# A graph layer on one core: order of the first loads, place of the weight transforms, one load and one sum on other engines

## The chip, the core and the metric

The kernel runs on one core of a Trainium2 chip. A core has TensorE (PE, with weight loads shown apart as PEld), VectorE (DVE), ScalarE (ACT), GpSimd (POOL) and SyncE (SP), all running their own instruction streams in order and waiting for each other by semaphores. DMA transfers are issued from SP, ACT and POOL. The metric is the device time of one execution in microseconds (us), as the median of several runs; lower is better.

## The reference, cut to what is computed

```
h = relu(layernorm(x))                        # x: 32 x 512 x 256 float32, adj: 32 x 512 x 512
hc = relu(bn(conv1d(h, conv1_w, width 1)))    # over channels
x_conv = relu(bn(conv1d(hc, conv2_w, width 17)) + h)
s = h @ w_se.T + b_se                         # 3 numbers per node
A = exp(-|s_n - s_m|^2) * adj
x_nmp = A @ relu(h @ w_msg.T + b_msg)
gi = [x_conv, x_nmp] @ w_ih.T + b_ih          # 3*256 outputs: r, z, n
gh = h @ w_hh.T + b_hh
r, z = sigmoid(gi_r + gh_r), sigmoid(gi_z + gh_z)
out = x + (1 - z) * tanh(gi_n + r * gh_n) + z * h
```

## The kernel before, in words

The 32 batches are worked in two groups of 16 (`GB`). Each group has a first part and a nodes part, and after both groups the gates follow for 16 pairs of batches.

**First part** (`first_part`). For each batch: load x; row statistics on VectorE (`statistics`, L375 to L380) and a power on GpSimd (L381); `normalise` (L394, on VectorE in group 0 and mostly in group 1); `transpose_h`, eight transposes on TensorE (phT, L402) and relu out of PSUM (L406), with a store to DRAM (hd, L407); `conv1` (pc, L422) with the batch norm's shift added on VectorE (L425) and a relu on ScalarE (L426); and `windows_to_freq` (px, L437), which takes the batch before into the frequency domain, because the 17 wide convolution is done by Fourier transforms over windows of 64 tokens. In program order a batch b does the statistics of b + 2, the transposes of b + 1, xn of b + 2, conv1 of b and px of b - 1.

In group 0 the weights of that convolution are transformed as well, in 32 steps of `weights_to_freq`. A step is four matmuls (pw, L346) of 17 x 80 weights and 512 columns, one on each group of 32 rows of the array, whose four PSUM banks are copied to tiles wst by ScalarE (L356) and VectorE (L354). After every second step four stores (wd, L360) go out on SP. Four steps share a tile w2p of taps, of which there are two buffers, filled by `load_taps` (L333, L334), from GpSimd's queue after the first. Which steps a batch does, and where, `between` says: it hands out a list for each of three places, before `normalise`, behind `conv1` and behind px. In the kernel before, a batch from 2 on has one step at the first place and one at the second; batch 6 has a third one behind px; batch 0 has two behind its conv1, and batch 1 one.

`between` also issues one entry of the list `load_weights` per batch, from batch 1 on: the back matrix of the inverse transform (L296), the message weights and biases, the vectors (`load_vectors`, L236, and `vectors`, L242 to L254 on GpSimd) and a scaling on GpSimd (L293).

All PSUM tiles come from one ring of eight banks (`bank`), in program order: a new tile waits until the tile eight places before has been read.

The order of each engine is the program's own (`manual_schedule`). Each DMA transfer from SP and ACT takes the next of eight semaphores in turn, and its issue waits until the transfer that had the semaphore before has landed. In the kernel before, x_0 comes in four transfers, two on SP and two on ACT, after vec on ACT; then on SP four of w1 (L199), x_1 (L203), five of the taps; and on ACT taps and fwd (L1267, L1268).

**Group 1's first part** has no weight transforms. Instead it finishes four frequency units of group 0 (the list `left`, at five places called `fill`), and combines the gate weights (`combine_weights`, shown at L1236): a list of steps, one per batch from batch 17 on, each with sums on GpSimd and copies on ScalarE. The first step only loads w_hhT (four transfers on SP, L199); the second, at the next batch, reads it.

**Nodes part** (`nodes`): messages (pm, L537), the affinity matrix and its product with the messages (pn, L641 and L624), and the products in the frequency domain (py, L486).

**Gates.** Before the first pair, sums of blocks of the operands are made on GpSimd in the order `FIRST_ORDER` (`block_sum`, L782 and L784): those of part hn, then `inverse(0)`, which brings the convolution back (pc, L844) and leaves cp, and then those of part c, the first of which is t4, a difference of rows of cp into tnc. The product (pg, L879) `t4_1` is the fourth of the first pair and reads it.

The places that the change touches most are these:

```python
load_weights = [
    partial(nc.sync.dma_start, back, nc.inline_tensor(back_np, name="dft_back").ap()),
    partial(load_rows, wmsg[:, :, :D], w_msgT, nc.sync),
    ...
n = (3, 0, *(3 if b == 6 else 2 for b in range(2, GB)))[b]
mine = [[steps.pop(0)] for _ in range(n)]
if b % 2 == 0 and b // 2 + 1 < QI // PI:
    mine[b > 0].insert(0, partial(load_taps, gen, b // 2 + 1))
return (mine[0] + mine[1], mine[2:]) if b == 0 else mine
```

Of the kernel before, what the change touches and what calls it, by code (L numbers as in the profile page):

```python
# [15 lines left out]
P = 128  # L16
# [134 lines left out]
def gnn_layer(  # L151
# [15 lines left out]
    nc = tc.nc  # L167
# [5 lines left out]
    NC = N // P  # L173
    G = 3 * D
    W = N // V
    GB = P // W
# [113 lines left out]
    def scale_embedding():  # L290
# [2 lines left out]
            nc.gpsimd.tensor_scalar(t, t, float(np.sqrt(2.0)), None, op0=ALU.mult)  # L293

    load_weights = [
        partial(nc.sync.dma_start, back, nc.inline_tensor(back_np, name="dft_back").ap()),  # L296
        partial(load_rows, wmsg[:, :, :D], w_msgT, nc.sync),
        partial(load_rows, wmsg[:, :, D:], w_seT, nc.sync),
        partial(nc.sync.dma_start, bmsg[:, :D], b_msg.to_broadcast([P, D])),
# [1 line left out]
        load_vectors,  # L301
        vectors,
        scale_embedding,
    ]


# [370 lines left out]
    def combine_weights():  # L677

        steps, loads, begins = [], [], []
        for k, src in enumerate((w_hhT, w_ihT[D:], w_ihT[:D])):  # L680
# [1 line left out]
                       for n, m in ((4, G // 2), (9, P), (len(PRODUCTS) + 2, P)))  # L682
            rows = w.rearrange("p (c h) m -> p c (h m)", c=DC)
            load = (partial(nc.sync.dma_start, rows, src.rearrange("(c p) m -> p c m", p=P)) if k == 1 else
                    partial(load_rows, rows, src, nc.sync))
            steps.append([])

            a11, a21, a12, a22 = (
# [76 lines left out]
    def block_sum(p, name, part):  # L765
        if name in BLOCK_SUMS:
            x, op, y = BLOCK_SUMS[name]
            dst, x, y = (operand(p, v, part) for v in (name, x, y))
            op = ALU.add if op == "+" else ALU.subtract
        else:  # L770
            rows = list(PAIR_SUMS)

            def whole(v):
                if isinstance(v, int):
                    return CP[p][:, v] if part == "c" else HN[p][:, :, v]
                return TNC[0][:, rows.index(v)] if part == "c" else TN[0][:, rows.index(v)]

            (x, y), op = PAIR_SUMS[name], ALU.subtract
            dst, x, y = whole(name), whole(x), whole(y)
            if part == "hn":  # L780
                for k in range(2):
                    nc.gpsimd.tensor_tensor(dst[:, k], x[:, k], y[:, k], op=op)  # L782
                return
        nc.gpsimd.tensor_tensor(dst, x, y, op=op)  # L784

    def sums_ahead(p, part):
        for name in SUMS_AHEAD:
# [464 lines left out]
    with tc.tile_pool(name="freq", bufs=1) as fpool:  # L1252
# [3 lines left out]
        with phase("first", "gen"):  # L1256
            gen = pools["gen"]
            per = N // D
            steps = [partial(weights_to_freq, gen, pc, i) for pc in range(QI // PI) for i in range(0, PI, per)]

            X[0] = pools["first"].tile([P, NC, D], FP, tag="x", name="x_0", bufs=3)
            for c in range(NC):
                (nc.sync if c % 2 == 0 else nc.scalar).dma_start(X[0][:, c, :], x[0, c * P : (c + 1) * P, :])
            load_w1()
            load_x(1)
            load_taps(gen, 0, nc.sync)
            nc.scalar.dma_start(taps, nc.inline_tensor(taps_np, name="dft_taps").ap())  # L1267
            nc.scalar.dma_start(fwd, nc.inline_tensor(fwd_np, name="dft_fwd").ap())  # L1268

            def between(b):  # L1270
                if 1 <= b <= len(load_weights):
                    load_weights[b - 1]()

                n = (3, 0, *(3 if b == 6 else 2 for b in range(2, GB)))[b]
                mine = [[steps.pop(0)] for _ in range(n)]
                if b % 2 == 0 and b // 2 + 1 < QI // PI:
                    mine[b > 0].insert(0, partial(load_taps, gen, b // 2 + 1))
                return (mine[0] + mine[1], mine[2:]) if b == 0 else mine

            with tc.manual_schedule():  # L1280
                xf = first_part(0, freq_tile, between)
# [109 lines left out]
        with phase("pw", "ahead"):  # L1391
            with phase("seven", "nodes"):
                with tc.manual_schedule():
                    nodes(0, xf, range(UNITS - LEFT), GB, range(UNITS - LEFT, UNITS - LEFT + 2))
            with phase("first", "sums"):
                combine = combine_weights()

                def between(b):

                    if b == GB - 3:  # L1400
                        for u in range(3):
                            load_unit(1, u)
                    two = [partial(sum_unit, pools["pw"], 1, b - GB + 3)] if b - GB + 3 >= REAL else []
                    return combine[b - 1] if 0 < b <= len(combine) else [], two


                pw, (u0, u1, u2, u3) = pools["pw"], range(UNITS - LEFT, UNITS)
                left = [[partial(load_unit, 0, u2, pools["sums"]), partial(prepare, pw, 0, u1, xf)],
                        [partial(product, pw, 0, u0, xf), partial(prepare, pw, 0, u2, xf)],
                        [partial(product, pw, 0, u1, xf), partial(load_unit, 0, u3)],  # L1410
                        [partial(prepare, pw, 0, u3, xf), partial(product, pw, 0, u2, xf)],
                        [partial(product, pw, 0, u3, xf)]]
                prepare(pw, 0, u0, xf)
                with tc.manual_schedule():
                    xf = first_part(1, freq_tile, between, left)
            with phase("seven", "nodes"):
                with tc.manual_schedule():
                    nodes(1, xf, range(UNITS), GB - 3)
# [92 lines left out]
```

## Time and profile before

| | before |
|---|---|
| median of 3 runs (range), us | 1768.27 (1766.25 to 1769.55) |
| profiled execution: time, us | 1769.15 |
| its span, first to last instruction, us | 1767.4 |
| mean granted clock of TensorE | 0.996 |
| TensorE busy, us (share) | 1752.5 (99%) |
| VectorE, ScalarE, GpSimd busy, us | 1338.3, 674.4, 1110.6 |
| first part of group 0, until the last px ends, us | 161 |
| first part of group 1, from its first transposes to the last px, us | 436 to 552 |
| first gate product, us | 844 |

The profile is of one execution. A line of the timeline gives the start and the length of a run of like instructions in us, the engine (SPq, ACTq and POOLq issue DMAs), the line of the kernel, the operation, what it writes and reads, how many, and in brackets how long the engine had been idle and what ended that. TensorE's matmuls overlap, so the start of one run of matmuls to the start of the next is the better measure of what it costs than the length shown.

### The profile page before, as it was taken

What the parts mean: (1) busy time and instruction counts of PE and PEld (TensorE: products, weight loads), DVE (VectorE), ACT (ScalarE), POOL (GpSimd) and SP (SyncE); (2) the same over time, 40 slices, a digit from 0 to 9 for tenths busy, and PEclk for the clock granted to TensorE, in tenths of its full rate; (3) what the DMA queues carried; (4) which work ended last, traced back from release to release, by engine and by line L of the source; (5) the groups of instructions that cost most, each with busy time, mean ns of one, the idle gap of its engine ahead of it and who ended that gap; (6) DMA issues with size and microseconds to landing.
All of it is one profiled execution on the core that took longest, in us unless ns stands there. A gap on an engine that the chain in (4) does not pass through costs nothing.

```text
span 1767.4 us, 24501 instructions
## 1 busy us (share of the span) xinstructions
PE 1752.5 (99%) x8046; PEld 1355.0 (77%) x8046; DVE 1338.3 (76%) x2617; ACT 674.4 (38%) x1543; POOL 1110.6 (63%) x1086
## 2 busy tenths in 40 slices
PE   9999999999999999999999999999999999999998
PEld 6777888888898888886877787778777787778754
DVE  7885888877896778876487778777877688777867
ACT  4556545543446445444322232323223232323221
POOL 3341786888554788777867556755766566755551
PEclk9999999999999999999999999999999999999999
DMA  8998988995778988888523553345423552345333
GB/s 230 317 299 230 259 216 236 232 240 175 257 267 213 260 229 238 227 239 275 177 67 64 120 126 95 75 81 125 117 66 69 126 126 72 68 111 125 102 60 71
DMA packets 311314, 295.16 MB, mean 167 GB/s; under 512 B 146940, under 2 KB 240668, under 8 KB 310804
## 3 DMA queue, kind: packets, MB, share of 16 engines
q1 hardware_dynamic: 301012, 265.77, 56.9%
q0 software_dynamic: 6736, 25.86, 4.6%
q10 hardware_dynamic: 3440, 1.97, 0.4%
q8 instruction: 64, 1.05, 0.2%
q14 instruction: 62, 0.51, 0.1%
HBM read 194.39 MB, written 99.16 MB: 166 GB/s over the span
## 4 chain that ended last, share of the span: by engine, by line
PE 94%; DMA 2%; DVE 1%; POOL 1%; SPq 1%; ACT 0%; issue 0%; ACTq 0%; POOLq 0%; DVEq 0%
PE pg L879 28%; PE pn L896 16%; PE py L486 12%; PE pn L641 10%; PE pm L537 6%; PE pc L422 5%; PE pc L844 5%; PE px L437 3%; PE pd L579 2%; PE pw L346 2%; PE phT L402 1%; PE pg L896 1%; PE pz L896 1%; PE psr L561 1%; DMA adj<-in_adj_dram 0%; DMA w<-in_w_hhT_dram 0%
## 5 line engine op out<-in xcount | busy, mean ns | idle before, releaser
L453 POOL TENSOR_TENSOR wsum<-wt 128x512 f32<-128x512 f32 x76 | 108.7, 1431 | 93.9 <-DMA wt<-wd 51.2
L486 PE MATMUL py<-wt,xf 128*128 128x256 f32 x640 | 154.2, 384 | 0.0
L879 PE MATMUL pg<-te,sw 128*128 128x256 f32 x600 | 154.0, 379 | 0.0
L486 PEld LDWEIGHTS py<-wt,xf 128*128 128x128 f32 x640 | 117.1, 190 | 34.9 <-issue 19.7
L870 ACT ACTIVATE rz<-rz,brz 128x256 f32<-128x256 f32 x180 | 86.4, 504 | 147.3 <-DVE rz L885 147.3
L589 DVE TENSOR_TENSOR A<-A,at 128x512 f32<-128x512 f32 x124 | 138.7, 1157 | 1.0 <-ACT A L585 0.9
L879 PEld LDWEIGHTS pg<-te,sw 128*128 128x128 f32 x600 | 114.0, 190 | 15.5
L879 PE MATMUL pg<-tn,sw 128*128 128x256 f32 x480 | 123.2, 379 | 0.0
L879 PE MATMUL pg<-hn,sw 128*128 128x256 f32 x480 | 123.2, 379 | 0.0
L896 PE MATMUL pn<-tn,sw_n 128*128 128x512 f32 x256 | 120.3, 592 | 0.0
L422 PE MATMUL pc<-w,hT 128*128 128x256 f32 x512 | 119.0, 386 | 0.5 <-DVE hT L406 0.5
L537 PE MATMUL pm<-wmsg,hq 128*128 128x259 f32 x512 | 117.5, 381 | 0.0
L1041 ACT ACTIVATE pn<-nt,vech 128x512 f32<-128x512 f32 x45 | 31.1, 692 | 218.7 <-DVE nt L1038 139.4
L422 PEld LDWEIGHTS pc<-w,hT 128*128 128x128 f32 x512 | 95.6, 192 | 24.0 <-issue 7.2
L782 POOL TENSOR_TENSOR tn<-hn 128x512 f32<-128x512 f32 x64 | 87.2, 1383 | 35.6 <-PE pn L896 35.6
L537 PEld LDWEIGHTS pm<-wmsg,hq 128*128 128x128 f32 x512 | 96.5, 189 | 14.7
L879 PEld LDWEIGHTS pg<-hn,sw 128*128 128x128 f32 x480 | 91.1, 190 | 18.3 <-issue 3.3
L381 POOL TENSOR_TENSOR rstd<-rstd,minus_half 128x4 f32<-128x4 f32 x32 | 33.3, 1041 | 112.8 <-DVE rstd L380 112.8
L879 PEld LDWEIGHTS pg<-tn,sw 128*128 128x128 f32 x480 | 91.2, 190 | 12.4
L885 DVE TENSOR_TENSOR ct<-pg,ct 128x256 f32<-128x256 f32 x180 | 74.7, 415 | 32.2 <-PE pg L879 22.6
L896 PEld LDWEIGHTS pn<-tn,sw_n 128*128 128x128 f32 x256 | 48.6, 190 | 61.2 <-issue 50.9
L844 PEld LDWEIGHTS pc<-back,yt 128*128 128x128 f32 x640 | 92.7, 190 | 1.3 <-issue 0.5
(225 smaller groups left out, 4428.9 us busy)
## 6 DMA issues: line engine op xcount, KB each, us to landing
wt<-wd SPq DMA_DIRECT2D x80, 512.0 KB, 7.0
adj<-in_adj_dram SPq DMA_DIRECT2D x128, 256.0 KB, 6.8
wd<-wst SPq DMA_DIRECT2D x64, 320.0 KB, 5.3
yd<-y SPq DMA_DIRECT2D x76, 256.0 KB, 6.2
yt<-yd SPq DMA_DIRECT2D x30, 640.0 KB, 5.8
hd<-hT SPq DMA_DIRECT2D x32, 512.0 KB, 5.3
nd<-nmp SPq DMA_DIRECT2D x32, 512.0 KB, 3.1
xb<-in_x_dram SPq DMA_DIRECT2D x128, 128.0 KB, 5.8
```

The lines of the kernel that those rows point to most:

```text
L422: nc.tensor.matmul(p[:, j, :], HT[b][:, ic, c * P : (c + 1) * P], w1[:, ic, :], start=(ic == 0), stop=(ic == DC - 1))
L453: nc.gpsimd.tensor_tensor(t, WT[g, u][:, 0], WT[g, u][:, 1], op=ALU.add)
L486: nc.tensor.matmul(dst, v[:, ic, :], w[:, ic, :], start=(ic == 0), stop=(ic == DC - 1))
L537: nc.tensor.matmul(p[:, : D + NS], hq[:, ic, c * P : (c + 1) * P], wmsg[:, ic, :], start=(ic == 0), stop=(ic == DC - 1))
L589: nc.vector.tensor_mul(A[b][:, mc, :], EXP.pop((b, mc)), AT.pop((b, mc)))
L641: nc.tensor.matmul(bk, left[:, k, :], right[:, k, :], start=(first and k == 0), stop=(k == 1), skip_group_check=True)
L782: nc.gpsimd.tensor_tensor(dst[:, k], x[:, k], y[:, k], op=op)
L844: nc.tensor.matmul(bk[:, t0:t1], YT[p][:, j, c, oc * P : (oc + 1) * P], back[:, n : n + t1 - t0], start=(c == 0), stop=(c == len(spans) - ...
L870: nc.scalar.activation(at(dst), at(src), AF.Sigmoid, bias=brz[:, o : o + 1], scale=sign)
L879: nc.tensor.matmul(bk, SW["hk"][:, k, s, :], c if k == 2 else hn[:, k], start=(onto is None and k == 0), stop=(k == K3 - 1), skip_group_ch ...
L885: nc.vector.tensor_tensor(at(dst), at(x), at(y), op=op)
L896: nc.tensor.matmul(bk[:, t], weight(q, k, o), terms[k][q][:, t], start=(first and i == 0), stop=(i == len(ks) - 1), skip_group_check=True)
```

## The change

The back matrix goes to the end of `load_weights`, so every other entry is issued one batch earlier. x_0 comes in three transfers instead of four, its second half as one, and taps and fwd are issued on SP behind the first taps load instead of on ACT. `between` hands out two steps at batch 0 instead of three (one behind conv1 of batch 0, one behind conv1 of batch 1), three at batch 11 besides batch 6, and from batch 3 on puts the first two steps of a batch together behind conv1, with nothing at the place before `normalise`; the load of taps stands between the two. The load of w_hhT is issued on GpSimd's queue and at the second `fill`, before unit 38's sums, instead of on SP at batch 17; the other steps of `combine_weights` stay at their batches. The t4 sum of part c of the first pair is done on VectorE.

```diff
     load_weights = [
-        partial(nc.sync.dma_start, back, nc.inline_tensor(back_np, name="dft_back").ap()),
         partial(load_rows, wmsg[:, :, :D], w_msgT, nc.sync),
...
         scale_embedding,
+        partial(nc.sync.dma_start, back, nc.inline_tensor(back_np, name="dft_back").ap()),
     ]
...
-                    partial(load_rows, rows, src, nc.sync))
+                    partial(load_rows, rows, src, nc.gpsimd if k == 0 else nc.sync))
...
-        nc.gpsimd.tensor_tensor(dst, x, y, op=op)
+        (nc.vector if (p, name, part) == (0, *FIRST_ORDER[ahead]) else nc.gpsimd).tensor_tensor(dst, x, y, op=op)
...
-            for c in range(NC):
-                (nc.sync if c % 2 == 0 else nc.scalar).dma_start(X[0][:, c, :], x[0, c * P : (c + 1) * P, :])
+            for queue, c0, c1 in ((nc.sync, 0, 1), (nc.scalar, 1, 2), (nc.sync, 2, NC)):
+                queue.dma_start(X[0][:, c0:c1, :], x[0, c0 * P : c1 * P, :].rearrange("(c p) d -> p c d", p=P))
             load_w1()
             load_x(1)
             load_taps(gen, 0, nc.sync)
-            nc.scalar.dma_start(taps, nc.inline_tensor(taps_np, name="dft_taps").ap())
-            nc.scalar.dma_start(fwd, nc.inline_tensor(fwd_np, name="dft_fwd").ap())
+            nc.sync.dma_start(taps, nc.inline_tensor(taps_np, name="dft_taps").ap())
+            nc.sync.dma_start(fwd, nc.inline_tensor(fwd_np, name="dft_fwd").ap())
...
-                n = (3, 0, *(3 if b == 6 else 2 for b in range(2, GB)))[b]
+                n = (2, 0, *(3 if b in (6, 11) else 2 for b in range(2, GB)))[b]
...
-                return (mine[0] + mine[1], mine[2:]) if b == 0 else mine
+                return (mine[0], mine[1:]) if b == 0 else mine if b < 3 else [[], mine[0] + mine[1], *mine[2:]]
...
-                    return combine[b - 1] if 0 < b <= len(combine) else [], two
+                    return combine[b - 2] if 1 < b <= len(combine) + 1 else [], two
...
-                        [partial(product, pw, 0, u0, xf), partial(prepare, pw, 0, u2, xf)],
+                        [*combine.pop(0), partial(product, pw, 0, u0, xf), partial(prepare, pw, 0, u2, xf)],
```

## The prediction

> **What bounds the kernel now.** I read the busy shares first, then TensorE's waits, then the timeline stage by stage.
>
> ```profile
> PE 1752.5 (99%) x8046; PEld 1355.0 (77%) x8046; DVE 1338.3 (76%) x2617; ACT 674.4 (38%) x1543; POOL 1110.6 (63%) x1086
> ```
> TensorE is busy to the end, so only TensorE time counts: its gaps (6.6 us in sum, all in a few places) and what its matmuls cost by their order. Two batches of the first part of group 0 and of group 1, TensorE alone:
>
> ```profile
> 98.98 3.72 PE L422 MATMUL pc<-w,hT 128*128 128x256 f32 x16
> 102.63 1.10 PE L346 MATMUL pw<-w2p,taps 17*80 17x512 f32 x8
> 103.66 2.44 PE L437 MATMUL px<-fwd,h 128*128 128x160 f32 x16
> 105.94 1.04 PE L402 MATMUL phT<-ident,xn 128*128 128x128 f32 x8
> 106.91 1.10 PE L346 MATMUL pw<-w2p,taps 17*80 17x512 f32 x8
> ```
> ```profile
> 493.36 3.62 PE L422 MATMUL pc<-w,hT 128*128 128x256 f32 x16
> 496.82 2.34 PE L437 MATMUL px<-fwd,h 128*128 128x160 f32 x16
> 498.99 1.04 PE L402 MATMUL phT<-ident,xn 128*128 128x128 f32 x8
> 499.87 0.38 PE L422 MATMUL pc<-w,hT 128*128 128x256 f32 x1
> ```
> From conv1 to conv1 a batch takes 107.94 - 98.98 = 8.96 us in group 0 (its next conv1 starts at 107.94) and 499.87 - 493.36 = 6.51 us in group 1, which has the same work without the two weight steps (pw). So a weight step standing alone costs 2.45/2 = 1.23 us. Its four matmuls sit on four row groups and run side by side; each streams 512 columns in two passes of 0.43 us (that is the spacing of the 512-column float32 passes of L624), 0.86 us. The other **0.37 us** is the passage from full-array matmuls into row groups and back.
>
> The start, and the two places later where TensorE waits on something the diff touches:
>
> ```profile
> 5.49 0.43 DVE L375 BATCH_NORM_STATS2 stats<-x 128x6 f32<-128x256 f32 x1 [1.06 <-DMA x<-in_x_dram]
> 5.49 1.75 SPq L333 DMA_DIRECT2D w2p<-in_w2T_dram  x4
> 16.97 2.59 PE L346 MATMUL pw<-w2p,taps 17*80 17x512 f32 x4 [1.01 <-DVE h L425]
> 19.49 1.57 PEld L402 LDWEIGHTS phT<-ident,xn 128*128 128x128 f32 x8 [1.58 <-ACT wst L356]
> ```
> ```profile
> 18.00:20.00 2.00, 2.00 (x6) 0.51 (x4) 0.00 (x0) 2.00 (x6) 0.00 (x0) 0.50 1.00 111
> 24.00:26.00 2.00, 2.00 (x10) 1.70 (x10) 0.80 (x3) 0.00 (x0) 1.03 (x1) 0.92 0.97 268
> ```
> ```profile
> 466.51 1.28 POOL L1236 TENSOR_TENSOR w<-w 128x128 f32<-128x128 f32 x3 [4.66 <-DMA w<-in_w_hhT_dram]
> 471.10 2.00 DVE L394 TENSOR_SCALAR xn<-x,mv,rstd 128x256 f32<-128x256 f32 x4 [3.54 <-POOL rstd L381]
> 471.80 0.70 PE L402 MATMUL phT<-ident,xn 128*128 128x128 f32 x2 [0.74 <-DVE xn L394]
> ...
> 848.01 1.26 POOL L784 TENSOR_TENSOR tnc<-cp 128x512 f32<-128x512 f32 x1
> 849.32 0.70 PE L879 MATMUL pg<-tnc,sw 128*128 128x256 f32 x2 [0.35 <-POOL tnc L784]
> ```
> In the first of these four, the last quarter of x_0 holds both the statistics and SP's taps load, which waits for its semaphore; then the second weight step waits for PSUM banks, and the transposes of batch 1 for the copies out of them. The windows (after the busy times: clock, DMA share, GB/s) show TensorE at half clock from about 17.5 to 24.3. In the last fence GpSimd sits 4.66 us on w_hhT, its next power is late, VectorE's normalisation behind it too, and TensorE pays.
>
> **What the Trainium skill says.** "TensorEngine Tiling (Array Packing)", Key Properties: changing the tiling mode drains TensorE. The trace agrees: 0.37 us per stay in row groups. "TensorE: Matmul & The Clock Gate", Part 1: too little activity in a free-running window of about 3.4 us halves the clock. Here it is half for 6.8 us, two such windows, after the sparse stretch at 14 to 17.5. "DMA: Bandwidth & Descriptors", Issuing engines are not separate DMA queues: all queues share 16 DMA engines, another queue only saves issue time. That fits: nothing below counts on more bandwidth.
>
> **Part 1, pairs behind conv1.** Every weight step stays, only the stays in row groups change. Before: one at batch 0 (two steps), one at batch 1, two in each of batches 2 to 15, one more at 6: 31. After: 1, 1 and 2 in batches 0 to 2, one pair in each of batches 3 to 15, one extra each at 6 and 11: 19. That pays only if the second step follows without a hole; at batch 0 of this trace it does until banks run out (passes at 14.51, 14.94 and 15.37). I count **13 x 0.373 = -4.85 us** for the pairs, and batch 11's extra step under part 2, where it comes from.
>
> What could open a hole: eight PSUM banks are handed out in turn. The second step of a pair gets the banks of the transposes and of conv1, so it needs VectorE's second addition (L425) within the first step's 1.03 us; that takes 0.69 and a signal, some 0.8 after conv1 in the trace. It fits if VectorE stands free. Per batch it does 1.39 + 0.36 + 0.17 (statistics), 1.29 (hT), 1.37 (xn), 1.37 (additions), 1.9 (copies) = 7.9 us of a new period of 8.96 - 0.37 = 8.59: tight. GpSimd's tap loads now come behind the pair: four issues 2.3 to 3.2, one 0.6, an x load 0.8 us, some 4.4 us, and the next batch's power stands behind them. Where a load waits for the second step of a pair (batches 4 and 6) I work out xn about 1.3 us late and a hole of 0.75 us; elsewhere none, and 0.55 at batch 3, where VectorE is still behind from the start. The stores of wst have 2 x 8.59 - 2.9 = 14.3 us from issue to reuse in the pair regime (11.6 before), but only 8.6 at batches 7 to 10, against some 3.5 to issue and 5.3 to land: I take 0.3 us. New holes: 0.55 + 0.75 + 0.75 + 0.3 = 2.35. Those after batch 2 of before go: 0.16 + 0.42 + 0.10 + 0.52 around 77 to 90 = 1.2. **Net +1.1**, between -1.2 (no new hole) and +3.3 (twice as many).
>
> **Part 2, the start.** x_0 in three transfers makes eight first loads, so none waits for one in flight. Its second half goes ahead of w1 on SP's queue; all of x_0 (0.5 MB at the 320 GB/s of 2.3 to 3.75) should be there at about 4.3 instead of 5.47. By the durations of the timeline: statistics 5.0, rstd 5.6, power 6.7, xn 8.1, transposes 9.1, conv1 9.8 to 13.4 (was 10.24 to 13.96). One weight step, no bank wait (1.01 gone). xn of batch 1 about 15.4 (x_1 landed at 11.9; I take 11.2), additions 16.7, hT 18.0: conv1 of batch 1 at 17.6 instead of 21.48. taps and fwd move from ACT's queue to SP's, two issues of 0.4 us behind the tap loads, which start at 3.9 instead of 5.49: still in time. x_2 now waits for x_1 to land (issue 11 instead of 8.04), read at 18: covered. Conv1 of batch 1 then ends at 21.4 at full clock, 24.6 if half clock comes again until 24.3, and about 23.0 if conv1's work ends it a window earlier, which I take. One step, the transposes and px to conv1 of batch 2: 29.2 instead of 34.0. That is 4.8 early with one step fewer done, which costs its 1.23 at batch 11: **-3.6 us**, between 0 and -5.5.
>
> **Part 3, back matrix last.** One 416 KB load on SP goes from batch 1 to batch 8, and wmsg, bmsg, vec2 (13 small issues) go one batch forward. The first reader of back is at 838 us, of wmsg at 161. GpSimd's vector work (2.3 us) goes one batch earlier, ahead of a power that isn't due. **0.**
>
> **Part 4, gate weights.** w_hhT goes from SP at 456.6 to GpSimd at about 442: four issues at the 0.53 of such loads, 2.2 us. It is read at 462, so the 4.66 us wait goes. The batch concerned lost (3.08 - 2.17) + (1.96 - 0.87) + (3.56 - 3.46) = **-2.1 us** against its neighbours. Queued behind the issues on GpSimd: wsum and both of unit 38 (done at 446.5 instead of 444.3, needed by TensorE at 446.85), a power, and unit 39 (needed at 450.3). **+0.3**, between 0 and 1.4 if the buffer or semaphore is late.
>
> **Part 5, first c sum on VectorE.** The t4 sum (1.26 us on GpSimd) goes to VectorE, idle from 845 to 851, and is there by about 846.3; the next sum on GpSimd comes 1.26 earlier. The start of the waiting product was 848.81 by the spacing of the passes and was 849.32: 0.51, plus some of the next. **-0.55**; -0.3 if r5 becomes the wait.
>
> **Sum:** -4.85 + 1.1 - 3.6 + 0 - 2.1 + 0.3 - 0.55 = -9.7 us. The profiled execution took 1769.15 us (span 1767.4), 0.9 above the median of 1768.27; 1759.4 for it, **1758.6 us** for the median.
>
> **Rivals.**
> (a) The start gives nothing: another load is last, and the half clock lasts as long as before. For it: five of the steps at the start follow landings that I only estimated. Against it: the bank wait and the copies go whatever lands. -9.7 + 3.6 = -6.1: 1762.2 us.
> (b) The DMA engines become the bound. 2.58 MB per batch (four wst stores, x, hT, half a tap set) in 8.59 us is 300 GB/s, and the DMA share is already 0.97. Against it: windows of 10 us reach 335 and 351. Stalls of 3 to 5 us more: about 1763 us.
> (c) Slower: **VectorE's additions decide the pair.** If xn, which stands before them, is late in every batch, the second step waits each time. Everything else brings 10.8 us; above 0.83 us a pair nothing is left, above 1.10 the kernel is over 0.2% slower. At 1.3 us (xn's own 1.37) it is 16.9 - 10.8 = +6: 1774 us. Against it: 0.7 us of slack per batch.
> (d) The pairs stay two stays, because the tap load or a wait between them empties the row groups: -9.7 + 4.85: 1763.4 us.
>
> **Chances.** Forecast 0.55, (a) 0.15, (b) 0.10, (d) 0.08, (c) in part, ending within 0.2%, 0.06, (c) in full 0.06. About 0.2%, 3.5 us, is what a measurement can tell from no change. Faster 0.83 (a twentieth of (a), (b) and (d) falls short), same 0.11, slower 0.06. Best ends: -5.5 - 4.85 - 1.2 - 2.1 - 0.55 = -14.2; worst without (c): 0 - 4.85 + 3.3 - 1.1 + 1.4 - 0.3 = -1.6. The range, 1754.5 to 1766, leaves out the tips of both and (c).
>
> **What would show it.** Right: pw in one group of 16 passes of about 1.9 us behind conv1, batches of 8.6 us, px of batch 15 some 7 us earlier; stats of x_0 done at 5; no wait on w_hhT near 462 and all batches of group 1 at 6.5; no TensorE wait on tnc. Wrong: waits of pw on DVE h in most batches, batches still at 8.96, half clock past 24 us, or waits of pg and py on GpSimd that weren't there.

## Result, and the profile after

The changed kernel is slower: 1770.4 us (median of 14 runs, 1767.66 to 1772.91) against 1767.37 us for the kernel before on the same chip, a ratio of **1.0017** (95% interval 1.0009 to 1.0024), or 3.0 us. The prediction was 9.7 us faster. The profiled execution took 1769.78 us, its span 1768.0.

The first line of the page shows nothing of it; TensorE is as full as before, and the busy time of every engine is within 6 us of what it was.

```profile
PE 1752.4 (99%) x8046; PEld 1356.8 (77%) x8046; DVE 1333.1 (75%) x2618; ACT 672.3 (38%) x1543; POOL 1107.1 (63%) x1089
```

The timeline of TensorE for one batch with a pair, where nothing disturbs it (batch 8):

```profile
89.82 3.62 PE L422 MATMUL pc<-w,hT 128*128 128x256 f32 x16
93.37 1.96 PE L346 MATMUL pw<-w2p,taps 17*80 17x512 f32 x16
95.36 2.44 PE L437 MATMUL px<-fwd,h 128*128 128x160 f32 x16
97.63 1.04 PE L402 MATMUL phT<-ident,xn 128*128 128x128 f32 x8
98.51 3.62 PE L422 MATMUL pc<-w,hT 128*128 128x256 f32 x16
```

The two steps are one group of 16 passes, and the batch takes 98.51 - 89.82 = 8.69 us. The start is earlier too. Conv1 of batch 1 stood at 21.48 and that of batch 2 at 34.00; now they start here, and the clock (first number after the busy times) stays whole where it was 0.50:

```profile
16.55 3.89 PE L422 MATMUL pc<-w,hT 128*128 128x256 f32 x16 [0.84 <-DVE hT L406]
27.70 3.62 PE L422 MATMUL pc<-w,hT 128*128 128x256 f32 x16
```
```profile
18.00:20.00 2.00, 2.00 (x11) 1.77 (x10) 0.85 (x7) 0.47 (x1) 0.97 (x1) 1.00 1.01 156
```

Yet the first pm of the nodes part starts at 163.46 in place of 160.98. Between conv1 of batch 2 and that pm, the changed kernel takes 135.76 us against 126.98. Measured from conv1 to conv1, batch 6 alone takes 16.37 us (10.30 before). From the timeline of batch 6, the lines of the chain, and three windows:

```profile
55.69 4.90 SPq L236 DMA_DIRECT2D vec<-in_vecs_dram  x4
63.09 3.62 PE L422 MATMUL pc<-w,hT 128*128 128x256 f32 x16
64.46 0.20 POOL L242 COPY vech<-vec 64x28 f32<-64x28 f32 x1 [7.62 <-DMA vec<-in_vecs_dram]
66.64 1.95 PE L346 MATMUL pw<-w2p,taps 17*80 17x512 f32 x12
67.16 1.02 POOL L381 TENSOR_TENSOR rstd<-rstd,minus_half 128x4 f32<-128x4 f32 x1
68.22 1.38 DVE L394 TENSOR_SCALAR xn<-x,mv,rstd 128x256 f32<-128x256 f32 x4 [2.70 <-POOL rstd L381]
69.52 1.28 DVE L425 TENSOR_TENSOR h<-pc,shift_row 128x512 f32<-128x512 f32 x2
70.26 2.27 PE L346 MATMUL pw<-w2p,taps 17*80 17x512 f32 x4 [1.67 <-DVE h L425]
72.46 4.64 PE L437 MATMUL px<-fwd,h 128*128 128x160 f32 x16
```
```profile
68.00:70.00 2.00, 0.59 (x4) 0.00 (x0) 1.78 (x5) 0.00 (x0) 0.18 (x1) 1.00 0.91 315
70.00:72.00 2.00, 1.74 (x4) 0.42 (x4) 1.99 (x4) 1.77 (x4) 0.00 (x0) 0.80 0.13 51
72.00:74.00 2.00, 2.00 (x7) 1.54 (x7) 0.69 (x1) 1.93 (x5) 1.17 (x3) 0.50 0.16 45
```

Read the chain in the order of time. GpSimd reaches the vector work (`vech`, L242) before vec2 has landed and stands for 7.62 us. The power of batch 8's statistics (L381) is behind it, xn behind the power, conv1's additions (L425) behind xn on VectorE. The second step of the pair needs the banks that those additions empty, so after 12 of its 16 passes the pair stands open (its passes no longer follow without a hole) for 1.67 us. Then the clock falls, and px takes 4.64 us where it took 2.44.

Before, the same work on GpSimd stood behind a taps load and an x load, and there was room for it:

```profile
68.36 3.11 SPq L236 DMA_DIRECT2D vec<-in_vecs_dram  x4
70.20 2.90 POOL L333 DMA_DIRECT2D w2p<-in_w2T_dram  x4 [0.30 <-PE pw L346]
73.70 0.81 POOL L203 DMA_DIRECT2D x<-in_x_dram  x1
74.50 0.51 POOL L242 COPY vech<-vec 64x28 f32<-64x28 f32 x2
80.58 1.02 POOL L381 TENSOR_TENSOR rstd<-rstd,minus_half 128x4 f32<-128x4 f32 x1 [3.47 <-DVE rstd L380]
```

At 74.50 GpSimd did not wait for vec2, and the power behind the vector work waited 3.47 us for its statistics.

The spans of the two profiled executions, 1767.4 and 1768.0 us, differ less than the medians. Each has 6.8 us of half clock ahead of the first pm: before from 17.5 to 24.3, changed from 71.2 to 78.0.

GpSimd's own waits in the first part of group 0 (us in total, times, longest):

```profile
POOL w2p L333 <- PE pw L346: 15.1, 4, 4.6
POOL vech L242 <- DMA vec<-in_vecs_dram: 7.9, 2, 7.6
```

The taps loads, which stand between the two steps of a pair, hold GpSimd until the pair has started, and the load of x comes behind them. So at batch 10 the statistics wait for x, and the pair opens (it takes 3.25 us for 1.96):

```profile
107.17 1.41 DVE L375 BATCH_NORM_STATS2 stats<-x 128x6 f32<-128x256 f32 x4 [1.12 <-DMA x<-in_x_dram]
...
110.75 3.25 PE L346 MATMUL pw<-w2p,taps 17*80 17x512 f32 x16
```

The two later places went much as the prediction has them. w_hhT is loaded from GpSimd at 445.46 and is there when it is read, and t4 is done on VectorE at 846.09, so that pg finds tnc ready:

```profile
445.46 2.19 POOL L199 DMA_DIRECT2D w<-in_w_hhT_dram  x4
465.10 1.38 POOL L1236 TENSOR_TENSOR w<-w 128x128 f32<-128x128 f32 x3
...
846.09 1.09 DVE L784 TENSOR_TENSOR tnc<-cp 128x512 f32<-128x512 f32 x1
...
849.97 0.59 PE L879 MATMUL pg<-tnc,sw 128*128 128x256 f32 x2
```
The sums behind the load are late once by the profile's count of TensorE's waits:

```profile
PE py L486 <- POOL both L466: 0.3, 1, 0.3
```

From start to start they cost more: conv1 to conv1 there takes 455.33 - 444.00 = 11.33 us, and took 452.08 - 441.67 = 10.41 before, so 0.9 us.

### The profile page after: what moved, and what is told of

It reads as the page before. It is cut to its first block, busy times and chain, and to the rows that moved or that the text cites. A ratio compares the mean times of both kernels' runs of the same rounds, so it can differ in the third digit from the quotient of the medians.

```text
span 1768.0 us, 24499 instructions
## 1 busy us (share of the span) xinstructions
PE 1752.4 (99%) x8046; PEld 1356.8 (77%) x8046; DVE 1333.1 (75%) x2618; ACT 672.3 (38%) x1543; POOL 1107.1 (63%) x1089
## 4 chain that ended last, share of the span: by engine, by line
PE 92%; DMA 2%; DVE 2%; ACT 1%; POOL 1%; issue 1%; SPq 1%; ACTq 0%; POOLq 0%; DVEq 0%
PE pg L879 29%; PE pn L896 16%; PE py L486 11%; PE pn L641 10%; PE pm L537 6%; PE pc L844 5%; PE pc L422 5%; PE px L437 3%; PE pd L579 2%; PE pw L346 1%; PE phT L402 1%; PE pg L896 1%; DMA x<-in_x_dram 1%; PE pz L896 1%; PE pn L624 1%; PE psr L561 1%
## 5 line engine op out<-in xcount | busy, mean ns | idle before, releaser
L589 DVE TENSOR_TENSOR A<-A,at 128x512 f32<-128x512 f32 x124 | 132.3, 1105 | 1.2 <-ACT A L585 1.1
L381 POOL TENSOR_TENSOR rstd<-rstd,minus_half 128x4 f32<-128x4 f32 x32 | 33.4, 1042 | 98.4 <-DVE rstd L380 98.4
```

What stands on the lines that cost most here:

```text
L589: nc.vector.tensor_mul(A[b][:, mc, :], EXP.pop((b, mc)), AT.pop((b, mc)))
```

## The experiments

The experiments test these theories:

- **V**: the vector entry comes a batch early and holds GpSimd.
- **X**: loads of x stand behind taps loads that wait for a pair.
- **E**: a third step leaves VectorE late for the next pair.
- **H**: an opened pair costs a second time, through half clock.
- **P**, the rival: pairs cost by themselves.

The table has each kernel's ratio to the kernel before, the mean granted clock over its runs, and from its profiled execution the batches (conv1 to conv1, us) and the start of the first pm. A batch with a third step has 1.2 us more by itself. In two expectations (taps moved; clean pairs without x) the batch called 4 or 5 has a number one too high against this table.

| kernel | ratio (95%) | clock | 4 | 6 | 7 | 10 | 11 | 12 | pm |
|---|---|---|---|---|---|---|---|---|---|
| before | 1 | 0.9977 | 8.96 | 10.30 | 10.00 | 8.95 | 8.96 | 8.96 | 160.98 |
| changed | 1.0017 (1.0009 to 1.0024) | 0.9958 | 9.63 | 16.37 | 10.36 | 10.01 | 9.88 | 9.91 | 163.46 |
| back first | 0.9998 (0.9990 to 1.0006) | 0.9973 | 8.95 | 10.60 | 12.01 | 9.86 | 9.87 | 9.91 | 158.93 |
| back last alone | 0.9998 (0.9989 to 1.0006) | 0.9975 | 8.96 | 10.30 | 9.17 | 8.96 | 8.96 | 8.95 | 157.41 |
| pairs alone | 0.9993 (0.9984 to 1.0002) | 0.9971 | 8.68 | 10.32 | 9.93 | 8.68 | 8.68 | 8.68 | 154.82 |
| start alone | 0.9993 (0.9985 to 1.0001) | 0.9984 | 8.96 | 10.40 | 8.95 | 8.95 | 10.30 | 9.17 | 155.78 |
| gates and sum alone | 0.9993 (0.9984 to 1.0001) | 0.9971 | 8.95 | 10.30 | 9.42 | 8.95 | 8.96 | 8.96 | 158.36 |
| changed, single steps | 0.9992 (0.9984 to 1.0000) | 0.9982 | 8.96 | 13.28 | 10.79 | 8.96 | 10.30 | 9.17 | 160.89 |
| back first, taps moved | 0.9996 (0.9988 to 1.0005) | 0.9970 | 12.01 | 9.87 | 12.00 | 8.69 | 10.29 | 11.58 | 162.54 |
| third step at 3, not 11 | 0.9981 (0.9975 to 0.9988) | 0.9975 | 12.71 | 9.87 | 9.96 | 8.69 | 8.68 | 8.68 | 156.65 |
| x early | 1.0008 (1.0002 to 1.0015) | 0.9963 | 8.69 | 17.14 | 10.23 | 8.69 | 9.87 | 9.87 | 162.04 |
| third steps last | 1.0031 (1.0020 to 1.0042) | 0.9954 | 9.71 | 14.97 | 8.69 | 12.03 | 8.69 | 8.68 | 164.43 |
| three edits | 1.0021 (1.0011 to 1.0031) | 0.9954 | 8.69 | 8.68 | 14.38 | 8.68 | 8.82 | 8.69 | 159.76 |
| three edits, taps moved | 0.9983 (0.9974 to 0.9991) | 0.9981 | 11.59 | 8.69 | 8.69 | 8.68 | 8.69 | 8.68 | 154.72 |
| hole filled | 0.9994 (0.9986 to 1.0002) | 0.9978 | 9.65 | 12.77 | 10.35 | 10.01 | 9.87 | 9.92 | 159.77 |
| clean pairs | **0.9966** (0.9953 to 0.9979) | 0.9983 | 8.68 | 9.86 | 8.68 | 8.69 | 9.86 | 8.68 | 152.57 |
| clean, without x | 0.9969 (0.9957 to 0.9981) | 0.9984 | 8.92 | 9.87 | 8.68 | 8.68 | 9.86 | 8.69 | 155.37 |
| clean, single steps | 0.9988 (0.9981 to 0.9994) | 0.9987 | 8.96 | 10.30 | 8.95 | 8.95 | 11.33 | 8.96 | 157.70 |

The experiments ran in four sets on three chips, each set beside the kernel before; so ratios are compared here, not times. The difference of two rows is known to some 2 us, with the first two rows of clean pairs to 2.5 or 3. The clock of before is the mean of 90 of its runs beside the first two sets; beside the other two it was 0.9975 and 0.9972. The batches are those of one execution of each kernel. Batch 8 of "clean, without x" took 11.95. 0.0001 of a ratio is 0.18 us.

### One part undone, or one part alone

The changed kernel with the list of before:

```diff
     load_weights = [
+        partial(nc.sync.dma_start, back, ...),
...
         scale_embedding,
-        partial(nc.sync.dma_start, back, ...),
```


> The changed kernel with the back matrix at the head of the list again, so every entry of it is issued at the batch of before. Theory V (the vector entry, one batch early, meets GpSimd before vec2 has landed; power, xn and additions of batch 6 are late, the pair opens and half clock follows): batch 6 (conv1 to conv1) falls from 16.4 us to 9.9 (8.7 and the third step), no half clock after 71 us, 1770.4 - 6.5 = 1764 us. Theory P (the pairs themselves cost it: VectorE's additions and loads of x behind the tap loads; the vector entry only marks the batch where it shows): another even batch takes over, 1768.5 to 1770.5 us.

Measured: batch 6 falls to 10.60, as V has it, and the kernel is 3.4 us faster (0.9998 for 1.0017; 1.4 to 5.3), about half of what V had. Half clock came back at 81 to 84 in the profiled execution, in batch 7, which now took 12.01. So V is the cause at batch 6, and not the only one.

The kernel before with the back matrix last:

```diff
     load_weights = [
-        partial(nc.sync.dma_start, back, ...),
...
         scale_embedding,
+        partial(nc.sync.dma_start, back, ...),
```

> The kernel before with the back matrix moved to the end of the list alone. Theory V: the wait of GpSimd on vec2 at batch 6 comes without pairs too (some 7 us, power late), and costs 2 to 6 us of TensorE time there: 1769.5 to 1773.5 us. Theory P: without pairs there is slack for it; within 1 us of the kernel before, 1766.5 to 1768.5 us.

Measured: no change, batch 6 as before. GpSimd does wait on vec2, 3.03 us, but the statistics that its power needs come 1.38 us after the vector work ends. V as I wrote it, a cost wherever GpSimd waits, falls; it needs a batch that starts earlier against the loads.

The kernel before with pairs:

```diff
-                return (mine[0] + mine[1], mine[2:]) if b == 0 else mine
+                return (mine[0] + mine[1], mine[2:]) if b == 0 else mine if b < 3 else [[], mine[0] + mine[1], *mine[2:]]
```

> The kernel before with the pairs behind conv1 from batch 3 on alone (steps per batch, start, list and loads as before). Theory V: batches of 8.7 us and, in three or four of them, 1 to 1.7 us more (statistics late behind a late load of x): 13 x (8.96 - 8.69) = 3.5 saved, some 4 lost, so 1766.5 to 1769 us, and batch 6 under 10.5 us. Theory P: a stall of 5 us or more in one even batch, 1771 us or more.

Measured: no batch over 10.32, and 8.68 or 8.69 from batch 8 to 13; -1.2 us (-2.8 to +0.4), at the edge of V's range (against the kernel before, -0.9 to +1.6). P falls. The difference to the changed kernel at batches 10 to 12 is in GpSimd's waits: with the steps counted as before, a taps load waits for a pair twice (6.8 us) and no longer after batch 6, against four times (15.1 us).

The kernel before with the new start (the first loads as in the change's diff, and):

```diff
-                n = (3, 0, *(3 if b == 6 else 2 for b in range(2, GB)))[b]
+                n = (2, 0, *(3 if b in (6, 11) else 2 for b in range(2, GB)))[b]
...
-                return (mine[0] + mine[1], mine[2:]) if b == 0 else mine
+                return (mine[0], mine[1:]) if b == 0 else mine
```

> The kernel before with the start of the changed kernel alone: x_0 in three transfers, taps and fwd on SP, two steps at batch 0 in place of three and three at batch 11; single steps as before. If the start gives what the trace of the changed kernel shows (conv1 of batch 2 at 27.7 in place of 34.0, 1.23 given back at batch 11): -5.1 us, 1762.3 us. If the gain is only lent (the clock or a later load takes it back before batch 6): 1766 to 1768 us.

Measured: -1.2 us (-2.7 to +0.2). Against the kernel before that is far from the first figure and in the second range (-1.4 to +0.6), but its reason, a gain that is taken back, is not what the trace shows. Conv1 of batch 2 starts at 27.13. But other kernels that keep the start of before have it at 30.73 (pairs alone), 31.25 (back last) and 31.97 (gates): the 34.00 of the profile that I predicted from was a long one, with half clock for 6.8 us where these have none, 3.4 and 3.4. Some 4 us are gained, batch 11 gives 1.35 back, and batch 2 takes 9.91 for 8.85.

The kernel before with w_hhT on GpSimd and t4 on VectorE (the four lines of the change's diff from `load_rows, rows` to `combine.pop(0)`):

```diff
-                    partial(load_rows, rows, src, nc.sync))
+                    partial(load_rows, rows, src, nc.gpsimd if k == 0 else nc.sync))
...
```

> The kernel before with w_hhT on GpSimd's queue at the second fill and t4 on VectorE alone. By the trace of the changed kernel 1.85 gained near 462 and 0.6 near 849: 2.0 to 2.5 us under the kernel before. If the gain is eaten by the late sums of unit 38 or by later waits: within 0.7 us of it.

Measured: -1.2 us (-2.8 to +0.2). The interval holds what the two first traces give for these two places (-2.1 + 0.9 - 0.65 = -1.85) and 0.7 as well.

The changed kernel with single steps:

```diff
-                return (mine[0], mine[1:]) if b == 0 else mine if b < 3 else [[], mine[0] + mine[1], *mine[2:]]
+                return (mine[0], mine[1:]) if b == 0 else mine
```

> The changed kernel with single steps at the places of before from batch 3 on (all else as changed, the back matrix last too). Theory I (each part alone saves or is neutral; the loss comes only where pairs meet the step put off to batch 11 and the early vector entry): start -1.2 as run alone, gate weights and sum -2, back 0: 3 to 4 us under the kernel before, no batch over 10.5. Theory V (the vector entry costs wherever GpSimd waits on it): no better than before, 0 to +2 us, batch 6 some 13 us.

Measured: -1.4 us (-2.8 to 0), between the figures of the two theories. GpSimd waits 7.57 us on vec2 as in the changed kernel, and batch 6 takes 13.28 in the profiled execution, so V cost there without pairs too, once the start is earlier. But that execution is one of the two slowest of 13, and eight of the others had a clock of 0.999, so the half clock seldom followed. The four parts alone sum to -4.0 us, give or take 3; together they give +3.0.

### What opens a pair

The taps loads out of the pair (and the back matrix first):

```diff
-                if b % 2 == 0 and b // 2 + 1 < QI // PI:
+                if b in (0, 2):
                     mine[b > 0].insert(0, partial(load_taps, gen, b // 2 + 1))
+                first = []
+                if b > 3 and b % 2 and b // 2 + 1 < QI // PI:
+                    first = [partial(load_taps, gen, b // 2 + 1)]
...
-                ... [[], mine[0] + mine[1], *mine[2:]]
+                ... [first, mine[0] + mine[1], *mine[2:]]
```


> The changed kernel with the back matrix first and, from batch 4 on, each taps load at the place before normalise of the next odd batch, behind that batch's load of x, no longer between the two steps of a pair. Theory X (a load of x that stands on GpSimd behind a taps load that waits for the pair makes statistics, xn and additions late): batches 4, 10 and 12 fall from 9.4, 9.9 and 9.9 to 8.7, and with no stretch of late additions batch 7 falls from 12.0 to 9 to 10: 5 us under the run with the back matrix first, some 5 us under the kernel before. Theory E (VectorE has too little slack in a pair, and a third step at 6 and 11 is what it can't make up): batches 7 and 12 stay at 10 or more, at most 1.5 us gained.

Measured: batch 10 is 8.69, as X has it, but the pairs of 7 and 12 still open (12.00 and 11.58), as E has it, and so does that of batch 4, where the statistics wait 2.32 us for x_6:

```profile
45.80 1.41 DVE L375 BATCH_NORM_STATS2 stats<-x 128x6 f32<-128x256 f32 x4 [2.32 <-DMA x<-in_x_dram]
```
Its load, issued at 36.35, still stands behind the taps load of batch 2, which the edit leaves where it was, and takes over 9 us to land.

The third step of batch 11 at batch 3:

```diff
-                n = (2, 0, *(3 if b in (6, 11) else 2 for b in range(2, GB)))[b]
+                n = (2, 0, *(3 if b in (3, 6) else 2 for b in range(2, GB)))[b]
```

> The changed kernel with the step that was put off done at batch 3 in place of batch 11 (one number in the edit: 11 becomes 3), so the taps loads wait for the first step of a pair or for none, as in the run with pairs alone. Theory X with D (the step put off makes the taps load wait for the second step): batches 10 and 12 at 8.7, stores before the vector loads end earlier on SP, so GpSimd waits under 5 us on vec2 and batch 6 is under 13 us: 4 to 6 us under the changed kernel. Theory E: batch 4 pays at once for the third step (10 us or more), batch 6 and 7 as in the changed kernel: within 1.5 us of it.

Measured: 6.4 us faster than the changed kernel, with batches 10 to 12 at 8.68 or 8.69 and a batch 4 of 12.71. So X with D (a step put off makes the taps loads wait for a second step) is right, and E is right at batch 4. The wait on vec2 is still 6.43 us, not under 5, but batch 6 now starts at 66.93 and the power at 67.06 comes early enough for it: again the place in time decides, not the wait.

Loads of x one batch earlier in the changed kernel:

```diff
-            if b + 3 < b1:
-                load_x(b + 3, nc.sync if b < 3 else nc.gpsimd)
+            for ahead in ((3,) if g or b < 3 else (3, 4) if b == 3 else (4,)):
+                if b + ahead < b1:
+                    load_x(b + ahead, nc.sync if b < 3 else nc.gpsimd)
```


> The changed kernel with the loads of x from x_7 on issued one batch earlier (at the head of batch b the load of x_{b+4}; the buffer is free by then), nothing else. Theory X (statistics wait for an x whose load stood on GpSimd behind a taps load): the waits of statistics on x at batches 4 and 10 go, both batches fall to 8.7, 2 to 4 us under the changed kernel; batch 6 (vector entry) and 12 (after a third step) keep their holes. Rival theory M (the DMA engines are full, an earlier issue only delays the taps, stores or vec2): the holes move to other batches, within 1 us of the changed kernel.

Measured: batches 4 and 10 at 8.69, and 6, 7 and 12 open as in the changed kernel. X holds for the batches, and the holes did not move as M has it. The total, 1.6 us faster (-0.2 to 3.3), can't tell the two apart.

Third steps at 14 and 15:

```diff
-                n = (2, 0, *(3 if b in (6, 11) else 2 for b in range(2, GB)))[b]
+                n = (2, 0, *(3 if b in (14, 15) else 2 for b in range(2, GB)))[b]
```

> The changed kernel with the two third steps moved from batches 6 and 11 to 14 and 15, where VectorE has no statistics and no xn; nothing else. Theory E (a third step leaves VectorE late, and in a pair lateness opens the next batch): batches 7 and 12 fall from 10.4 and 9.9 to 8.7 to 9, batches 6 and 11 lose their third step; 3 to 5 us under the changed kernel, while the wait on vec2 at batch 6 stays (13 us or more). Theory V alone: only what the moved step did beside it, within 1.5 us of the changed kernel.

Measured: batches 7 and 12 at 8.69 and 8.68, so E holds for the batches; but the whole is no faster (1.0031). Batch 10 opened to 12.03, and from the first pm to its end the profiled execution, the slowest of eight, takes 1610.3 us where that of the changed kernel takes 1604.5.

Three edits together: third steps at 14 and 15, x early as above, and the back matrix between the loading and the use of the vectors; then the same with the taps moved as above:

```diff
         load_vectors,
+        partial(nc.sync.dma_start, back, ...),
         vectors,
         scale_embedding,
-        partial(nc.sync.dma_start, back, ...),
```

> The changed kernel with three edits: x one batch earlier, third steps at 14 and 15, the back matrix between the loading and the use of the vectors (so they are used at batch 7 as before). If the three causes (late x, third step, vec2) are all there is: batches 3 to 13 at 8.7, first pm at 152 to 153 in place of 163.5, no half clock until the end, 8 to 10 us under the kernel before. If a pair opens for another reason: at least one batch over 10, first pm over 155.

> The same three edits, and the taps loads at the place before normalise of the next odd batch, so that nothing on GpSimd waits for a pair. If a waiting taps load still matters with x early: 1 us or more under the version without this edit. If x early has already taken its harm away: the same within 0.7 us.

Measured: with all three, batch 7 took 14.38, and this time GpSimd waited on no vector:

```profile
69.94 2.17 POOL L333 DMA_DIRECT2D w2p<-in_w2T_dram  x4 [5.17 <-PE pw L346]
72.10 0.61 POOL L334 DMA_DIRECT2D w2p<-in_w2T_dram  x1
72.70 0.81 POOL L203 DMA_DIRECT2D x<-in_x_dram  x1
73.50 0.51 POOL L242 COPY vech<-vec 64x28 f32<-64x28 f32 x2
...
76.08 1.02 POOL L381 TENSOR_TENSOR rstd<-rstd,minus_half 128x4 f32<-128x4 f32 x1
```

The taps load waits 5.17 us for the pair; its issues, an x load and 2.6 us of vector work follow, and the power comes at 76.08 for statistics that were ready at 72.4. With the taps moved that goes, every batch from 5 to 13 takes 8.68 or 8.69, and 6.7 us are gained. That refutes "the same within 0.7 us".

### The half clock by itself

Two matmuls whose result is not used, ahead of the pair's second step at batch 6 (hT of batch 6 is kept for them):

```diff
             p = bank(f"pw_{pc}_{i}_{q}")
+            if fill and q == 0:
+                for _ in range(fill):
+                    nc.tensor.matmul(p, ident, HT[6][:, 0, :], start=True, stop=True)
...
+                if b == 6:
+                    mine[1] = [partial(mine[1][0], fill=2)]
```


> The changed kernel with two full-array matmuls of 512 columns (0.86 us each, their result is overwritten) ahead of the second step of the pair at batch 6, where TensorE stood 1.67 us for the additions; they bring nothing to the result. Theory H (the half clock after 71 us comes from the thin stretch before it, and is about half of the loss of batch 6): batch 6 falls from 16.4 to 13 to 13.5, mean granted clock up by 0.001 to 0.002, 2.5 to 3.5 us under the changed kernel. Rival (the clock falls for the pw passes or the DMA wait, whatever fills the hole): batch 6 at 16.5 to 17.5 with half clock as before, 0 to 1 us slower than the changed kernel.

TensorE at batch 6 and one window of it (lines of the kernel are 3 higher here):

```profile
67.58 1.98 PE L348 MATMUL pw<-hT,ident 128*128 128x512 f32 x4
...
69.50 1.90 PE L349 MATMUL pw<-w2p,taps 17*80 17x512 f32 x8
71.45 2.44 PE L440 MATMUL px<-fwd,h 128*128 128x160 f32 x16
```
```profile
70.00:72.00 2.00, 1.95 (x12) 0.77 (x7) 2.00 (x4) 2.00 (x5) 0.30 (x1) 1.00 0.03 12
```

Measured: the additions are nearly as late (68.98, 5.97 us after conv1 began, for 6.43), GpSimd waits 7.25 us on vec2, and batch 6 still falls by 3.6 us, to 12.77: the clock stays at 1.00 and px is back at 2.44. The mean clock of the runs rises from 0.9958 to 0.9978, and the kernel is 4.1 us faster (2.1 to 6.0; I gave it 2.5 to 3.5). H is shown at batch 6. An estimate from the clocks fits the whole result: against the four sets' 0.9972 to 0.9977 for the kernel before, the changed kernel lacks 0.0014 to 0.0019 of 1768 us, 2.5 to 3.4 us of full clock, and it is 3.0 us slower.

### Clean pairs

The vectors used at batch 7 and the taps moved, as above; x early, from x_6 on; and the third steps' copies on ScalarE. The second kernel leaves x as it was, the third has single steps:

```diff
+            for ahead in ((3,) if g or b < 2 else (3, 4) if b == 2 else (4,)):
...
-            if (pc or i >= SI) and (q == 3 or (q == 1 and s == 0)):
+            if not by_scalar and (pc or i >= SI) and (q == 3 or (q == 1 and s == 0)):
...
                 mine = [[steps.pop(0)] for _ in range(n)]
+                mine[2:] = [[partial(m[0], by_scalar=True)] for m in mine[2:]]
```


> The changed kernel with the vectors used at batch 7, x one batch early from x_6, taps loads at the place before normalise of the next odd batch, and the copies of the third steps at 6 and 11 all on ScalarE. Theory E in its fine form (the harm of a third step is its copies on VectorE): batches 6 and 11 at 9.9, all others from 4 to 13 at 8.7, first pm near 151.5, no half clock between 30 and 160; 7 to 9 us under the kernel before. If a third step opens the next pair for another reason (banks, ScalarE late): batch 7 or 12 over 9.7, 3 to 6 us under the kernel before.

> As the version of clean pairs, without the earlier loads of x. If taps loads out of the way are enough: within 1 us of it. If an x whose load is issued at the head of the batch lands after 7 to 8 us as at batch 5 of the run with the taps moved: a batch among 4 and 5 at 11 to 12, 2 to 4 us slower than it.

> As the version of clean pairs, with single steps from batch 3 on (one before normalise, one behind conv1). If the pairs' gain exists once nothing opens them: 13 x 0.27 = 3.5 us slower than clean pairs (batches at 8.96 for 8.69), so 4 to 5 us under the kernel before. If the pairs bring nothing even then: the same within 1 us.

TensorE of clean pairs at batch 6, third step included:

```profile
66.50 1.96 PE L346 MATMUL pw<-w2p,taps 17*80 17x512 f32 x16
68.48 2.44 PE L437 MATMUL px<-fwd,h 128*128 128x160 f32 x16
70.85 1.10 PE L346 MATMUL pw<-w2p,taps 17*80 17x512 f32 x8
71.88 1.09 PE L402 MATMUL phT<-ident,xn 128*128 128x128 f32 x8
```

Measured: 1759.78 us, 6.0 us under the kernel before by the ratio (3.7 to 8.3) and the best of all, with batches 7 and 12 at 8.68. So the harm of a third step was its copies on VectorE ("back first, taps moved" has them there and has 11.58 at batch 12; "clean, without x", which differs from it in little else, has 8.69). Where they are on ScalarE, VectorE begins the statistics behind them 3.35 us before the next conv1 (69.46 and 72.81); in the changed kernel, after batch 11's third step, it was 0.11 (126.97 and 127.08). The 6.0 is under the 7 to 9 expected, whose lower part the interval holds; the first pm is at 152.57. Without x early the profiled execution has one open batch, 8, and 2.8 us more to the first pm; in the medians the two can't be told apart. With single steps the same kernel is at 0.9988: clean pairs are 0.0022, 3.9 us, faster (1.3 to 6.5). Not all of it need be the pairs. The profiled execution with single steps has two long batches of its own, 11 with 11.33 us and 13 with 9.73, 1.8 us over the 10.30 and 8.96 of its other ones; in the first a step waits 0.76 us for taps that land late. The batches that nothing disturbs give 13 x 0.27 = 3.5 us for the pairs.

Left open: third steps at 14 and 15 brought less in the total than in the batches. In their profiles half clock comes again after the first part, between 174 and 186 or at 458; in the one with the taps moved eight wd stores in a row hold SP from 149.02 to 157.49. Whether that is the cause was not tried.

## Why the prediction was wrong, point by point

- **Part 3, the step that failed**: "GpSimd's vector work (2.3 us) goes one batch earlier, ahead of a power that isn't due. 0." The power was due: its statistics were done at 64.3 in the trace, and it came at 67.16, because the work ahead of it waited for its own input. I took the place of the work from before, where the taps load and x load stood in front of it, and did not ask when vec2 lands. In the changed kernel SP issues it from 55.69 to 60.59, behind the four wst stores of a pair, and batch 6 starts 6.6 us earlier (63.09 for 69.72). In the trace the step costs 16.37 - 8.69 - 1.19 (third step) = 6.5 us, of which filling the hole took away 3.6. In the medians it costs 3.4 us (back first). The prediction is off by 9.7 + 3.0 = 12.7 us, so this step is not all of it.
- **Holes in part 1**: predicted 2.35, less 1.2 that was to go: 1.1. Measured are 0.94 + 1.67 + 1.32 + 1.22 = 5.15 at batches 4, 7, 10 and 12, less the 1.04 that batch 7 had lost before (10.00 against 8.96): 4.1. I counted the loads that wait for the second step (4 and 6), and overlooked that the step put off to batch 11 lets the taps loads of 8 and 10 wait for a pair too, and that a third step makes VectorE late for the pair after it.
- **Stays in part 1**: the mechanism was right, the term too large: 8.96 - 8.69 = 0.27 a pair for 0.373. px now waits for copies out of the pair's first banks: from pw to px 1.99 us where 1.03 + 0.86 = 1.89 was meant, and its weight loads stand 0.89 us for ScalarE's copies. 13 x 0.27 = 3.5 for 4.85.
- **Part 2**: -3.6 predicted, -5.1 between the two traces (6.3 earlier, 1.2 given back), about -1.2 alone. The half clock from 17.5 to 24.3, which I took as a property of the kernel before, was one of that execution. The Trainium skill, "TensorE: Matmul & The Clock Gate", Part 1, warns of it for the first matmuls of a kernel: the window runs free, so how long they run slow varies from run to run. The traces agree: four kernels with the first loads of before had 6.8, 3.4, 3.4 and 0 us of half clock there. I cited that page for the window's length and not for this.
- **Parts 4 and 5** were right: the distance between the two traces falls by 2.1 where w_hhT was waited for (from 3.24 at conv1's 458.76 and 462.00 to 1.15 at 486.86 and 488.01; predicted 2.1) and by 0.65 near 849 (0.55). The sums behind the issues cost 0.9 for 0.3, inside the range of 0 to 1.4.
- **Rivals**: (c) named the mechanism, additions that decide the pair, but not its place. It is not xn in every batch, but in 5 of 13 pairs: a late power at 6, a late x at 4 and 10, and a third step's copies at 7 and 12. (d) did not happen: the taps load leaves the pair whole. (b) did not as it was put: the DMA share is 0.13 to 0.16 where TensorE suffers most. But the x that batch 10 waits for was issued at 97.65 and was there only at 107.17, at a share of 0.84 to 1.07, so busy DMA engines may have a part in the late x; that was not tried apart. (a) did not in the traces, where conv1 of batch 2 comes at 27.1 to 29.4 with the new start and at 30.7 to 34.0 with the old; the medians of the start alone can't exclude it.

## What to carry to other kernels

Before you price a moved instruction at nothing on an in-order engine, write down what stands in front of it and behind it at its new place, with the time at which its own input lands; 2.3 us of work that waited 7.6 us for its input, in front of a power that TensorE needs, cost 6.5 us in the trace. A tighter packing lives on the slack of the engines that feed it: pairs were worth some 3.5 us with it, and without it the changed kernel was 4.4 us slower than with single steps. And price a hole twice on this chip's TensorE: once for the wait, once for the clock that may follow.

## What the hardware showed that I had not expected

The clock halved though TensorE never stood still for long: the largest idle time in batch 6 before the clock fell at 71.2 was 1.67 us, between row-group passes. The Trainium skill, "TensorE: Matmul & The Clock Gate", HAM oscillation — how this bites in real kernels, puts its abstract rule as no idle gaps over some 3.4 us. The trace differs: here the clock fell after a thin stretch with a gap of half that, and with 1.98 us of matmuls in the gap it stayed whole, worth 3.6 us in that batch. Not every opened pair is followed by half clock: those of batches 4, 7, 10 and 12 in the same execution were not. A run's own mean clock shows it without a profile: of the runs of the changed kernel the four at 0.995 have a median of 1771.87 us, the seven at 0.996 of 1769.15.
